# First pair's features before attention, later pairs' features at row blocks' ends, in a two-layer graph attention kernel

## The chip, the cores and the metric

The kernel runs on one core of a Trainium2 chip. The core has five engines that run side by side, each working through its own instructions in order: PE (matrix multiply, with its weight loads shown apart as PEld), DVE (vector), ACT (activation functions), POOL (a slower general engine) and SP, which here only issues DMAs. They meet at semaphores. The metric is the device time of one execution in microseconds (us), the median of several runs.

## The reference

There are N = 4096 nodes with 512 columns each, and an adjacency matrix of 4096 x 4096 floats. Two layers of attention follow each other, both with a layer norm, a ReLU and a residual:

```
h = relu(layernorm(x))                       # no scale, no shift
d = (h @ W.T + b).reshape(N, 8, 64)          # features of 8 heads
src, trg = sum(d * src_proj), sum(d * trg_proj)        # [N, 8] each
e = leaky_relu(src[n] + trg[m]) + adj[n, m]            # per head, [N, N]
x = x + softmax(e) @ d                                 # layer 0

h = relu(layernorm(x))
k, q, v = h @ Wk, h @ Wq, h @ Wv             # 8 heads of 64
a = softmax(q k^T / 8 - 1e16 * (1 - max(adj, eye)))
x = x + sum over heads of (a @ v) @ Wo                 # layer 1
```

Everything is in fp32. Only layer 0 is touched by the change.

## The kernel before, in words

Heads are taken in pairs. Layer 0 handles the first three pairs (`PAIRS` = 3) in one loop and the fourth in a loop of its own, into which the projections of layer 1 are woven; then comes layer 1's attention and a last product with `Wo`. All loops are written out in the order in which each engine is to work (`manual_schedule`); tiles come from pools with a fixed number of buffers, and a tile waits until the one before it in its buffer is done with.

**The prologue** (L394 to L417) works in sets of four row blocks (512 nodes), eight sets, each step of a set one iteration behind the one before:
- `load_rows` loads 1 MB of `x` into one of three buffers, `moments` takes mean and variance on DVE.
- `normed` makes (x - mean) * rstd, half of it on DVE and half on POOL (L309).
- `turned_rows` turns it on PE (L321), and ACT takes it out of PSUM with a ReLU as `hT` (L324). All eight `hT` stay in SBUF for the features.
- `halves` needs no features: `prepared` has multiplied the weights with the projections into a small matrix `u` (16 columns), and `u` times `hT` gives the source and target half of every logit (L332, 16 rows by 512 columns). The target halves go to DRAM (`trg_d`) and come back spread over all partitions as `tb`; the source halves are turned into columns (`sources`, L346).
- at the end `turned_weights` turns the weights on PE into `wt`.

**The attention loop** (L425 to L464) takes a group, a block of 128 rows of one head pair, in two steps, one per head, and each step in two half steps. 96 groups make 192 steps. In a step n:
- `leaky` (ACT, L143) makes the 128 x 4096 leaky sums into a tile `t`; it is issued one step ahead, in half step 0.
- `masked` (DVE, L154) adds 2048 columns of `adj` per half step and takes the smallest (L159).
- `exps` (ACT, L164) follows one step behind, in half step 1.
- `turned` (PE, L177) transposes a quarter of the group per half step, `taken` copies it out of PSUM in two tiles, two of seven on ACT (L186), the rest on DVE (L188); `weighted` (PE, L199) multiplies the quarter of the half step before with the features. `LEAD` = 7 half steps lie between a step and its transposes; `t` has 7 buffers.
- `finish` ends a group in three further half steps: the sums are copied (L212), turned back on PE (L217), divided by the denominators and added to the block of `x` (L220, L223), and stored to `x1_d`.

The features of all pairs are made in the first eight half steps of that loop (`features`, L357, one set per half step, 256 matmul records in all), get their bias on DVE (`features_out`, L365) and go to DRAM as `d1_d` (L368). `load_feats` (L131) brings one pair's quarter at a time back into one of four buffers. SP issues all these DMAs in the written order, so that one that waits holds up those behind it.

Of the kernel before, what the change touches and what calls it, by code (L numbers as in the profile page):

```python
# [23 lines left out]
def kernel(  # L24
# [49 lines left out]
    x1_d = dram.tile([N, DM], F32, name="x1_d")  # L74
    qk_d = dram.tile([P, HC, 2, N], F32, name="qk_d")
# [12 lines left out]

    CH = 2048
# [6 lines left out]
    LEAD = 7  # L96
    with tc.tile_pool(name="a0k", bufs=1) as pk, tc.tile_pool(name="a0v", bufs=4) as pv, tc.tile_pool(
        name="a0a", bufs=3
    ) as pa, tc.tile_pool(name="a0t", bufs=7) as pt, tc.tile_pool(name="a0p", bufs=4) as pp, tc.tile_pool(
        name="a0x", bufs=1  # L100
    ) as px, tc.tile_pool(name="a0s", bufs=4) as psb, tc.tile_pool(
# [3 lines left out]
        class Group:  # L105


            def __init__(self, c, g):
                self.c, self.g = c, g
                self.t = {}  # L110
                self.nm = {}
                self.pT = {}

# [78 lines left out]
        def weighted(G, i):  # L192
            if i == 0:
                G.o = po.tile([P, 2 * P], F32, name="o")
            for b in range(MB):
                mb = i * MB + b
                pT = G.pT[i, b // 4]
                for h in range(2):
                    nc.tensor.matmul(  # L199
                        G.o[h * D : (h + 1) * D, :P],  # L200
                        lhsT=feats[G.c][i][:, b, bass.ts(h, D)],
                        rhs=pT[:, bass.ts(b % 4 * 2 + h, P)],
                        start=(mb == 0), stop=(mb == NB - 1),
                    )

        def finish(G):

            rows, cols = bass.ts(G.g, P), bass.ts(G.c, PR)
            xt = px.tile([P, PR], F32, name="xt")
            nc.sync.dma_start(xt, x[rows, cols])  # L210
            oT = px.tile([P, P], F32, name="oT")
            nc.vector.tensor_copy(oT, G.o[:, :P])  # L212
            den = psb.tile([P, 2], F32, name="den")
            nc.vector.reciprocal(den, G.sm)
            yield
            back = G.o[:, P:]
            nc.tensor.transpose(back, oT, ident)  # L217
            yield
            att = px.tile([P, 2, D], F32, name="att")
            nc.vector.tensor_mul(  # L220
                att, back.rearrange("p (h d) -> p h d", d=D), den.unsqueeze(2).to_broadcast([P, 2, D])
            )
            nc.gpsimd.tensor_add(xt, xt, att.rearrange("p h d -> p (h d)"))  # L223
            nc.sync.dma_start(x1_d[rows, cols], xt)

        XR = CH // DM
        u = px.tile([P, P], F32, tag="oT", name="u")[:, : KC * 2 * H].rearrange("p (c k) -> p c k", c=KC)
# [16 lines left out]
        def prepared(wn, col):  # L244


            by_head = px.tile([P, 2, D], F32, tag="att", name="by_head").rearrange("p a d -> p (a d)")
            by_head = by_head[:, : HC * 2 * H].rearrange("p (c k) -> p c k", c=HC)
            nc.vector.memset(by_head, 0.0)
            for c in range(HC):  # L250
                for half in range(2):
                    rows = bass.ts(half, D)
                    at = 2 * c + half
                    nc.vector.tensor_copy(by_head[rows, c, at : at + H + 1 : H], col[rows, 0:2, c])
            up = ptr.tile([P, TW], F32, tag="tr", name="up")
            for kc in range(KC):
                for c in range(HC):
                    nc.tensor.matmul(
                        up[:, bass.ts(kc, 2 * H)], lhsT=wn[c // 2][:, c % 2, bass.ts(kc, P)], rhs=by_head[:, c],
                        start=(c == 0), stop=(c == HC - 1),  # L260
                    )
            for c in range(HC):
                nc.tensor.matmul(
                    up[: 2 * H, 512:513], lhsT=by_head[:, c], rhs=col[:, 2, c : c + 1],
                    start=(c == 0), stop=(c == HC - 1),
                )
            nc.vector.tensor_copy(u.rearrange("p c k -> p (c k)"), up[:, : KC * 2 * H])
            nc.vector.tensor_copy(cs[: 2 * H], up[: 2 * H, 512:513])

        def turned_weights(wn):  # L270
            wt = []
            for j in range(KC // 2):
                tp = ptr.tile([P, TW], F32, tag="tr", name="wtp")
                for i in range(2):
                    for c in range(HC):
                        nc.tensor.transpose(
                            tp[:, bass.ts(i * HC + c, P)], wn[c // 2][:, c % 2, bass.ts(j * 2 + i, P)], ident
                        )
                wt.append(pv.tile([P, 2, HD], F32, tag="v", name="wt"))
                nc.scalar.copy(wt[j].rearrange("p k o -> p (k o)"), tp)  # L280
            return wt
# [21 lines left out]
        def normed(R):  # L303
            nc.vector.reciprocal(R.rstd, R.rstd)
            R.hn = []
            for r in range(XR):
                if r % 2 == 0:
                    R.hn.append(pp.tile([P, 2, DM], F32, tag="pT", name="hn"))
                (nc.gpsimd if r % 2 else nc.vector).tensor_scalar(  # L309
                    R.hn[-1][:, r % 2], R.x[:, r], R.mv[:, r, 0:1], R.rstd[:, r], ALU.subtract, ALU.mult  # L310
                )

        def turned_rows(R, q):
# [3 lines left out]
            for j in range(XR // 2):  # L317
                tp = ptr.tile([P, TW], F32, tag="tr", name="htp")
                for r in range(2):
                    for kc in range(KC):  # L320
                        nc.tensor.transpose(  # L321
                            tp[:, bass.ts(r * KC + kc, P)], R.hn[j][:, r, bass.ts(kc, P)], ident
                        )
                nc.scalar.activation(  # L324
                    R.hT[:, bass.ts(j, 2)].rearrange("p r k n -> p (r k n)"), tp, AF.Relu
                )

        def halves(R, q):

            lp = ptr.tile([P, TW], F32, tag="tr", name="lp")  # L330
            for kc in range(KC):
                nc.tensor.matmul(  # L332
                    lp[: 2 * H, : XR * P], lhsT=u[:, kc], rhs=R.hT[:, :, kc, :],
                    start=(kc == 0), stop=(kc == KC - 1),
                )
            R.lr = pp.tile([P, TW], F32, tag="pT", name="lr")
            nc.vector.tensor_scalar(
                R.lr[: 2 * H, : XR * P], lp[: 2 * H, : XR * P], cs[: 2 * H], None, ALU.add
            )
            nc.sync.dma_start(trg_d[:, bass.ts(q, XR * P)], R.lr[H : 2 * H, : XR * P])  # L340

        def sources(R, q):

            sp = po.tile([P, 2 * P], F32, tag="o", name="sp")
            for r in range(XR):
                nc.tensor.transpose(  # L346
                    sp[:, bass.ts(r, H)], R.lr[:H, bass.ts(r, P)], ident[:H, :H]
                )
            nc.vector.tensor_copy(
                src[:, bass.ts(q, XR), :].rearrange("p n h -> p (n h)"), sp[:, : XR * H]  # L350
            )

        def features(R, q, j):
            tp = ptr.tile([P, TW], F32, tag="tr", name="mp")
            for r in range(2):
                for kc in range(KC):
                    nc.tensor.matmul(  # L357
                        tp[:, bass.ts(r, HD)], lhsT=R.hT[:, j * 2 + r, kc, :], rhs=wt[kc // 2][:, kc % 2, :],
                        start=(kc == 0), stop=(kc == KC - 1),
                    )  # L360
            return tp

        def features_out(q, j, tp):
            d1 = pp.tile([P, 2, HD], F32, tag="pT", name="d1")
            nc.vector.tensor_add(  # L365
                d1, tp.rearrange("p (r o) -> p r o", r=2), bb.unsqueeze(1).to_broadcast([P, 2, HD])
            )
            nc.sync.dma_start(  # L368
                d1_d[bass.ts(q * XR // 2 + j, 2 * P), :].rearrange("(r p) d -> p r d", p=P), d1
# [23 lines left out]
        with tc.manual_schedule():  # L393
# [5 lines left out]
            for q in range(NQ + 4):  # L399
                if q + 2 < NQ:  # L400
                    rows.append(load_rows(q + 2))
                if q < NQ:
                    moments(rows[q])
                if q == 1:
                    prepared(wn, col)
                if 0 <= q - 1 < NQ:
                    normed(rows[q - 1])
# [10 lines left out]
            wt = turned_weights(wn)  # L418
            bb = pk.tile([P, HD], F32, name="bb")
            nc.sync.dma_start(bb, b0.partition_broadcast(P))  # L420
# [4 lines left out]
            for s in range(total + 6):  # L425
                G, h = step(s) if s < total else (None, 0)
                for half in range(2):
# [8 lines left out]
                    q = 2 * s + half  # L436
                    made = [(q, j, features(rows[q], q, j)) for j in range(XR // 2)] if q < NQ else []
                    if q == NQ + 1:
                        sources_by_sets()
                    if half == 0 and s + 1 < total:  # L440
# [5 lines left out]
                    if half == 1 and 0 <= s - 1 < total:  # L446
                        exps(*step(s - 1))
                    if s < total:
                        masked(G, h, half)
                    for each in made:  # L450
                        features_out(*each)
                    if q < NQ and q % 2:
                        load_feats(0, q // 2)
# [4 lines left out]
                    if 1 <= n <= 2 * total:  # L458
                        W, w = groups[(n - 1) // HALVES], (n - 1) % HALVES
                        weighted(W, w)  # L460
                        if W.g == NB - 1 and W.c + 1 < PAIRS:
# [629 lines left out]
```

## Time and profile before

| what | us |
|---|---|
| median of 3 runs | 5093.84 (5091.9 to 5098.46) |
| the profiled execution | 5095.06 |
| its span, first to last instruction | 5093.2 |
| prologue, to the first `leaky` | 92.57 |
| from there to the fourth `exps` | 120.97 |
| last weighted sum of layer 0's loop starts | 1802.07 |
| busy in the whole span: PE, DVE, ACT, POOL | 4812.7, 4541.1, 3928.1, 376.7 |

A row of a timeline gives start, duration, engine, line, operation, output and inputs, shapes and how many were merged; in brackets the idle time of the engine before it and what ended it. Durations of neighbouring instructions overlap at their ends, so the distance from one start to the next is the better price. A row of a group list gives line, engine, operation, tiles, shapes, count, then busy us and mean ns of one, then the idle time before them. One fp32 matmul makes two records on PE.

### The profile page before, as it was taken

To read this page: it belongs to the slowest core of one execution; us is meant where nothing else is said; L and a number is where in the kernel's file an instruction comes from. 1 tells how busy PE (TensorE), PEld (TensorE's weight loads), DVE (VectorE), ACT (ScalarE), POOL (GpSimd) and SP (SyncE) were. 2 spreads that over 40 slices of the span, in tenths; PEclk is the share of its full clock that TensorE was granted. 3 is DMA by queue.
4 is the path that set the end of the run, shared out by engine and by line. 5 is a ranking of instruction groups with operands and counts; after the bars stand their busy time and mean duration, and the time that the engine had idled before them with its cause. 6 is when DMAs were issued, how large, how long until landed. Compare 5 with 4: busy or idle time off the path is not lost.

```text
span 5093.2 us, 145280 instructions
## 1 busy us (share of the span) xinstructions
PE 4812.7 (94%) x61850; PEld 3471.2 (68%) x61850; DVE 4541.1 (89%) x8125; ACT 3928.1 (77%) x4581; POOL 376.7 (7%) x632
## 2 busy tenths in 40 slices
PE   7999999999999959999989999999999999999999
PEld 3588888888888847677756666666666666666664
DVE  4599999999999989888759999999999999999971
ACT  3499999999999988888748888666666666666651
POOL 2000000000000011111112222000000000000000
PEclk9999999999999979999999999999999999999999
DMA  4344353344443364444367777544343343533325
GB/s 157 129 142 140 127 190 132 134 142 169 147 142 128 126 161 136 138 142 138 107 205 239 240 239 239 167 128 127 126 159 126 125 126 128 157 125 126 127 94 178
DMA packets 316152, 764.83 MB, mean 150 GB/s; under 512 B 54448, under 2 KB 156848, under 8 KB 290416
## 3 DMA queue, kind: packets, MB, share of 16 engines
q1 hardware_dynamic: 314976, 754.49, 46.1%
q8 instruction: 486, 7.96, 0.7%
q14 instruction: 162, 1.33, 0.1%
q10 hardware_dynamic: 528, 1.05, 0.1%
HBM read 629.41 MB, written 125.96 MB: 148 GB/s over the span
## 4 chain that ended last, share of the span: by engine, by line
PE 55%; DVE 20%; ACT 14%; issue 7%; DMA 4%; SPq 1%; POOL 0%; DVEq 0%; ACTq 0%; POOLq 0%
PE o L937 18%; PE sc L856 18%; DVE t L154 6%; DVE pT L188 6%; PE tr L920 6%; ACT t L143 4%; ACT t L164 3%; DVE bt L557 3%; PE oo L1058 2%; ACT pT L186 2%; PE mp L357 2%; PE tr L177 2%; DVE bt L596 2%; PE o L199 2%; ACT bt L589 1%
## 5 line engine op out<-in xcount | busy, mean ns | idle before, releaser
L872 DVE CUSTOM_DVE_ANT_0 t<-sc,a 128x512 f32<-128x512 f32 x2048 | 1291.4, 686 | 77.3 <-issue 55.3
L907 ACT ACTIVATE t<-t,nm 128x1024 f32<-128x1024 f32 x1024 | 1168.5, 1143 | 163.7 <-DVE nm L896 163.7
L937 PEld LDWEIGHTS o<-t,v 128*64 128x64 f32 x16384 | 883.9, 137 | 423.7 <-issue 337.7
L856 PE MATMUL sc<-k,q 64*32 64x512 f32 x16384 | 1003.1, 597 | 9.4 <-DVE nm L872 9.4
L937 PE MATMUL o<-t,v 128*64 128x128 f32 x16384 | 1007.1, 276 | 0.2 <-ACT oT L947 0.2
L914 DVE STREAM_TRANSPOSE t<-t 128x1536 f32<-128x1536 f32 x512 | 908.2, 1774 | 8.9 <-ACT t L907 5.9
L154 DVE CUSTOM_DVE_ANT_0 t<-t,a 128x2048 f32<-128x2048 f32 x384 | 876.5, 2282 | 18.0 <-DMA a<-in_adj_dram 18.0
L177 PE MATMUL tr<-ident,t 128*128 128x128 f32 x6144 | 782.6, 277 | 103.3 <-ACT pT L186 91.9
L164 ACT ACTIVATE t<-t,nm 128x4096 f32<-128x4096 f32 x192 | 786.7, 4097 | 27.5 <-DVE nm L159 27.5
L143 ACT ACTIVATE t<-tb,src 128x4096 f32<-128x4096 f32 x192 | 786.2, 4096 | 19.0 <-PE mp L357 17.4
L177 PEld LDWEIGHTS tr<-ident,t 128*128 128x128 f32 x6144 | 664.0, 141 | 198.8 <-ACT pT L186 115.1
L199 PE MATMUL o<-pT,v 128*64 128x128 f32 x12288 | 757.1, 276 | 0.3 <-DVE pT L188 0.3
L199 PEld LDWEIGHTS o<-pT,v 128*64 128x64 f32 x12288 | 664.4, 137 | 64.0 <-issue 63.0
L188 DVE COPY pT<-tr 128x1024 f32<-128x1024 f32 x549 | 657.4, 1217 | 40.4 <-PE tr L177 33.5
L926 ACT COPY t<-tr 128x512 f32<-128x512 f32 x512 | 299.1, 584 | 483.4 <-PE tr L920 478.6
L856 PEld LDWEIGHTS sc<-k,q 64*32 64x32 f32 x16384 | 251.2, 106 | 342.0 <-issue 299.6
L920 PE MATMUL tr<-ident,t 128*128 128x128 f32 x2048 | 342.7, 287 | 10.9 <-ACT t L907 9.2
L547 ACT ACTIVATE lk<-tb,srcb 128x1024 f32<-128x1024 f32 x256 | 281.9, 1112 | 80.8 <-DVE nm L557 73.9
L186 ACT COPY pT<-tr 128x1024 f32<-128x1024 f32 x219 | 302.6, 1382 | 52.1 <-DMA d_d<-d 36.1
L596 DVE STREAM_TRANSPOSE bt<-bt 128x2048 f32<-128x2048 f32 x128 | 295.1, 2306 | 30.0 <-ACT bt L589 30.0
L557 DVE CUSTOM_DVE_ANT_0 bt<-lk,ba 128x1024 f32<-128x1024 f32 x256 | 302.1, 1215 | 22.0 <-ACT e L681 11.2
L589 ACT ACTIVATE bt<-bt,nm 128x1024 f32<-128x1024 f32 x256 | 290.3, 1135 | 0.4 <-DVE nm L578 0.3
(113 smaller groups left out, 3911.2 us busy)
## 6 DMA issues: line engine op xcount, KB each, us to landing
a<-in_adj_dram SPq DMA_DIRECT2D x192, 1024.0 KB, 5.6
a<-pen_d SPq DMA_DIRECT2D x384, 512.0 KB, 3.8
ba<-in_adj_dram SPq DMA_DIRECT2D x512, 128.0 KB, 2.9
a<-in_adj_dram SPq DMA_DIRECT2D x512, 128.0 KB, 3.3
pen_d<-a SPq DMA_DIRECT2D x128, 512.0 KB, 3.4
qk_d<-e SPq DMA_DIRECT2D x64, 256.0 KB, 2.2
x<-in_x_dram SPq DMA_DIRECT2D x8, 1024.0 KB, 5.7
d_d<-d SPq DMA_DIRECT2D x16, 512.0 KB, 2.9
```

What stands on the lines that cost most here:

```text
L143: nc.scalar.activation(t, targets[G.c, h], AF.Prelu, bias=src[:, G.g, 2 * G.c + h : 2 * G.c + h + 1], alpha=SLOPE)
L154: nc.vector.tensor_tensor_reduce(out=t, in0=t, in1=rows_of_adj[G, f], scale=-1.0, scalar=FMAX, op0=ALU.add, op1=ALU.min, accum_out=nm[:, f ...
L164: nc.scalar.activation(G.t[h], G.t[h], AF.Exp, bias=G.nm[h][:, NCH : NCH + 1], scale=-1.0, accum_out=G.sm[:, h : h + 1],)
L177: nc.tensor.transpose(tr[:, bass.ts(b % 4 * 2 + h, P)], G.t[h][:, bass.ts(i * MB + b, P)], ident)
L188: nc.vector.tensor_copy(pT, tr)
L199: nc.tensor.matmul(G.o[h * D : (h + 1) * D, :P], lhsT=feats[G.c][i][:, b, bass.ts(h, D)], rhs=pT[:, bass.ts(b % 4 * 2 + h, P)], start=(mb ...
L856: nc.tensor.matmul(sc[h][bass.ts(a, SQ), :], lhsT=G.q[bass.ts(h, D), bass.ds(G.q0 + k * SQ, SQ)], rhs=keys[G.c][half][bass.ts(h, D), a, :] ...
L872: nc.vector.tensor_tensor_reduce(out=t[:, G.ring + k, h, cols], in0=scs[half][h], in1=a[:, cols], scale=1.0, scalar=FMAX, op0=ALU.add, op1 ...
L907: nc.scalar.activation(u, u, AF.Exp, bias=G.nm[k // 2][:, k % 2, h : h + 1], scale=-1.0, accum_out=G.sm[:, k, h : h + 1],)
L914: nc.vector.transpose(u, u)
L920: nc.tensor.transpose(tr[:, bass.ts(h * NT + m, P)], t[:, G.ring + k, h, bass.ds(VC + m * P, P)], ident)
L937: nc.tensor.matmul(G.o[bass.ts(h, D), :P], lhsT=v[:, b, bass.ts(h, D)], rhs=t[:, bass.ds(G.ring, GS), h, bass.ds(at, SQ)], start=(mb == 0) ...
```

## The change

- **Features.** The eight `hT` are also stored to DRAM (`hT_d`), in the prologue. The first pair's features (128 of 512 columns) are made in the prologue, one set per iteration (`first_features`), and stay in SBUF. Those of the next pair are made during a pair's groups: `finish` multiplies one row block's `hT`, loaded back from DRAM (`load_rows_turned`), with 128 columns of `wt` right after the turn back, adds the bias and stores the 128 x 128 result to `d1_d`. Groups 0 and 1 of a pair do two blocks, groups 30 and 31 none.
- **Weights.** `turned_weights` moves to the second iteration of the prologue; `wt` and the bias get tiles of their own.
- **Logit halves.** `u` gets 32 columns per chunk (16 of them zero). Each of the four row blocks of a set has its own column tile of PE: 16 matmuls of 128 columns into 32 PSUM rows each, instead of 4 of 512 columns. One transpose makes the sources instead of four; four small stores write the targets instead of one.
- **Normalization.** All four blocks of a set go to POOL, as x * rstd + shift instead of (x - mean) * rstd; DVE makes the shift column.
- **Order.** `leaky` moves from half step 0 to 1 and `exps` from 1 to 0; `LEAD` and the buffers of `t` go from 7 to 6. The sources of the last pair are spread in step 1 instead of step 4.

```diff
-    LEAD = 7
+    LEAD = 6
...
-        name="a0t", bufs=7
+        name="a0t", bufs=6
...
+                self.blocks = [b for b in (g, NB - 2 + g) if b < (NB if g < 2 else NB - 2)]
...
+        def load_rows_turned(G):
+            G.hT = []
+            for b in G.blocks:
+                h = ph.tile([P, KC, P], F32, name="h")
+                nc.sync.dma_start(h, hT_d[b].rearrange("p (k n) -> p k n", k=KC))
+                G.hT.append(h)
...
             nc.tensor.transpose(back, oT, ident)
+            for i in range(len(G.blocks)):
+                for kc in range(KC):
+                    nc.tensor.matmul(
+                        G.o[:, bass.ts(2 + i, P)], lhsT=G.hT[i][:, kc, :], rhs=wt[:, kc, after],
+                        start=(kc == 0), stop=(kc == KC - 1),
+                    )
...
+            for i, b in enumerate(G.blocks):
+                d1 = px.tile([P, PR], F32, name="d1")
+                nc.vector.tensor_add(d1, G.o[:, bass.ts(2 + i, P)], bb[:, after])
+                nc.sync.dma_start(d1_d[bass.ts(b, P), after], d1)
...
-                (nc.gpsimd if r % 2 else nc.vector).tensor_scalar(
-                    R.hn[-1][:, r % 2], R.x[:, r], R.mv[:, r, 0:1], R.rstd[:, r], ALU.subtract, ALU.mult
+                nc.gpsimd.tensor_scalar(
+                    R.hn[-1][:, r % 2], R.x[:, r], R.rstd[:, r], R.shift[:, r], ALU.mult, ALU.add
...
+            nc.sync.dma_start(
+                hT_d[bass.ts(q, XR)].rearrange("r p k -> p r k"), R.hT.rearrange("p r k n -> p r (k n)")
+            )
...
             for kc in range(KC):
-                nc.tensor.matmul(
-                    lp[: 2 * H, : XR * P], lhsT=u[:, kc], rhs=R.hT[:, :, kc, :],
-                    start=(kc == 0), stop=(kc == KC - 1),
-                )
+                for r in range(XR):
+                    nc.tensor.matmul(
+                        lp[bass.ts(r, SQ), :P], lhsT=u[:, kc], rhs=R.hT[:, r, kc, :],
+                        start=(kc == 0), stop=(kc == KC - 1),
+                    )
...
+            for r in range(XR):
+                nc.sync.dma_start(
+                    trg_d[:, bass.ts(q * XR + r, P)], R.lr[r * SQ + H : r * SQ + 2 * H, :]
+                )
...
+        def first_features(R, q):
+            tp = ptr.tile([P, TW], F32, tag="tr", name="mp")
             for r in range(XR):
                 for kc in range(KC):
                     nc.tensor.matmul(
-                        tp[:, bass.ts(r, HD)], lhsT=R.hT[:, j * 2 + r, kc, :], rhs=wt[kc // 2][:, kc % 2, :],
+                        tp[:, bass.ts(r, PR)], lhsT=R.hT[:, r, kc, :], rhs=wt[:, kc, :PR],
...
+            nc.sync.dma_start(bb, b0.partition_broadcast(P))
-            for q in range(NQ + 4):
+            for q in range(NQ + 5):
...
+                if 0 <= q - 1 < NQ:
+                    normed(rows[q - 1])
                 if q == 1:
                     prepared(wn, col)
-                if 0 <= q - 1 < NQ:
-                    normed(rows[q - 1])
+                    turned_weights(wn)
...
-                    made = [(q, j, features(rows[q], q, j)) for j in range(XR // 2)] if q < NQ else []
-                    if q == NQ + 1:
+                    if (s, half) == (1, 0):
                         sources_by_sets()
-                    if half == 0 and s + 1 < total:
+                    if half == 0 and 0 <= s - 1 < total:
+                        exps(*step(s - 1))
+                    if half == 1 and s + 1 < total:
                         leaky(*step(s + 1))
...
-                    if half == 1 and 0 <= s - 1 < total:
-                        exps(*step(s - 1))
...
                         weighted(W, w)
+                        if w == 0:
+                            load_rows_turned(W)
```

## The prediction

> **What bounds the kernel now.** I read the busy times by stretch first. Columns: stretch, its length, then busy time and count on PE, PEld, DVE, ACT, POOL, then granted clock, DMA share, GB/s.
>
> ```profile
> 0.00:92.57 92.57, 66.10 (x286) 35.12 (x287) 43.31 (x118) 20.51 (x27) 37.27 (x23) 0.98 0.45 146
> 92.57:213.50 120.93, 115.60 (x311) 54.35 (x311) 42.53 (x40) 35.62 (x14) 0.00 (x0) 0.98 0.38 139
> 300.00:1740.00 1440.00, 1345.56 (x16689) 1203.43 (x16687) 1402.84 (x1622) 1440.00 (x718) 42.09 (x87) 1.00 0.41 144
> ```
>
> Three stages touch the change: a prologue without attention (to 92.57, the first leaky), a stretch in which PE is full and ACT works 36 of 121 us, and the steady attention of the first three pairs, in which ACT never rests. The rest of the span is another stage's code and is not touched. The timeline of ACT shows what the second stretch is:
>
> ```profile
> 92.57 10.91 ACT L143 ACTIVATE t<-tb,src 128x4096 f32<-128x4096 f32 x3 [1.62 <-DMA tb<-trg_d]
> 107.83 1.28 ACT L164 ACT_TABLE_LOAD   x1 [4.35 <-DVE nm L159]
> ...
> 145.33 3.72 ACT L143 ACTIVATE t<-tb,src 128x4096 f32<-128x4096 f32 x1 [6.22 <-PE mp L357]
> 162.78 3.71 ACT L164 ACTIVATE t<-t,nm 128x4096 f32<-128x4096 f32 x1 [13.73 <-DVE nm L159]
> ...
> 212.63 1.01 ACT L186 COPY pT<-tr 128x1024 f32<-128x1024 f32 x1 [36.12 <-DMA d_d<-d]
> 213.54 3.71 ACT L164 ACTIVATE t<-t,nm 128x4096 f32<-128x4096 f32 x1
> ```
>
> Up to the fourth exp (213.54) ACT waits for features (mp L357) and what is queued behind them. Last, the timeline of the steady state, where start-to-start distances are the real prices:
>
> ```profile
> 1005.08 4.12 ACT L164 ACTIVATE t<-t,nm 128x4096 f32<-128x4096 f32 x1
> 1007.52 2.28 DVE L154 CUSTOM_DVE_ANT_0 t<-t,a 128x2048 f32<-128x2048 f32 x1
> 1007.84 1.97 PE L177 MATMUL tr<-ident,t 128*128 128x128 f32 x16
> ...
> 1008.78 4.10 ACT L143 ACTIVATE t<-tb,src 128x4096 f32<-128x4096 f32 x1
> ...
> 1011.12 2.28 DVE L154 CUSTOM_DVE_ANT_0 t<-t,a 128x2048 f32<-128x2048 f32 x1
> 1011.63 1.97 PE L177 MATMUL tr<-ident,t 128*128 128x128 f32 x16
> 1012.39 1.39 ACT L186 COPY pT<-tr 128x1024 f32<-128x1024 f32 x1
> 1013.28 4.11 ACT L164 ACTIVATE t<-t,nm 128x4096 f32<-128x4096 f32 x1
> ...
> 1013.52 2.35 DVE L188 COPY pT<-tr 128x1024 f32<-128x1024 f32 x2
> ...
> 1015.78 2.28 DVE L154 CUSTOM_DVE_ANT_0 t<-t,a 128x2048 f32<-128x2048 f32 x1
> ...
> 1016.98 4.11 ACT L143 ACTIVATE t<-tb,src 128x4096 f32<-128x4096 f32 x1
> ```
>
> Per group (two steps, four half steps), with 8 tiles out of PSUM, 2/7 of them on ACT:
> - ACT: exp 3.70, leaky 3.61, copy 0.89: 2 x 7.31 + 2.29 x 0.89 = 16.65. The exps run at 8.33 a step, so ACT sets the pace.
> - DVE: four masks of 2.21, two minima of 0.19, 5.71 copies of 1.13 and 0.47 of ends: 16.15.
> - PE: a half step of transposes and weighted sums is 1011.63 - 1007.84 = 3.79: with the turn back (0.11) 15.27.
>
> **The change, part by part.**
>
> *Features out of the first half steps.* 256 matmul records of L357 (110.6 us busy, 0.43 each for 512 columns) and 16 additions leave. From the first leaky to the fourth exp ACT then has only its own work: six leakys 21.7, three exps 11.1, table 1.3, a copy 0.9 = 35.0, and one wait, as the first exp needs both masks of step 0. The first mask now starts 5.9 after the leaky, because the first adj tile lands then; two masks are 4.6 and the second tile costs another 1.5, so the exp can start at 12, where leaky 0 and 1 end at 7.2: 4.8. The set of sources moved ahead of step 1's masks is about 1.5 on DVE and lies in the slack of step 1's exp. So 40 instead of 121: **81 us gained**. The new order does the fourth exp before the sixth leaky; I count the same work on both sides.
>
> *The prologue.* PE per four row blocks: 16 transposes 1.90; logit halves; one transpose 0.3 instead of four; first features 32 records of 128 columns at 0.43/4 = 0.107, 3.4. The halves were 8 records of 0.43 = 3.4; now 32 of 0.107 in four column tiles. No row has this form. Bounds: side by side 0.9, one after another 3.4; L856 runs eight tiles at 0.061 a record of 0.43, seven at once, so I take 1.0. Together 6.7, with the changes of mode 6.8. DVE falls to 4.4 (moments 3.2, small ones 0.6, feature addition 0.6).
>
> POOL now does four normalizations per block set instead of two. Its rows differ in price by the pair of operations:
>
> ```profile
> L843 POOL TENSOR_SCALAR a<-a 128x1024 f32<-128x1024 f32 x128 | 134.7, 1053 | 466.8 <-ACT a L842 297.1 <-DMA a<-in_adj_dram 156.1 <-DMA pen_d<-a 5.2
> L654 POOL TENSOR_SCALAR bhn<-xr,bmv,brstd 128x512 f32<-128x512 f32 x32 | 66.1, 2073 | 110.8 <-issue 87.3 <-DVE brstd L650 23.5
> L731 POOL TENSOR_SCALAR wq<-wq 128x2048 f32<-128x2048 f32 x1 | 5.4, 5378 | 0.0
> ```
>
> Subtract-multiply with two columns as operands is 2.07 per 512 elements, one multiply 1.34, add-multiply with constants 0.53. The new pair, multiply-add with columns, is in no row: between 0.53 and 2.07. Here a rule of the Trainium skill bears (GPSIMD Engine Reference, section 3.1): a tight loop with one input needs about 1.8 cycles an element, 0.77 us for 512. L654's row is nearly three times that. What decides is 6.8/4 = 1.7 us: below it PE sets the prologue, and three of four prices lie below; I take that.
> - PE sets it: `up` ends near 26 as now (17.1 start, plus 16 more records for the column sums), the weights' transposes 29.5, at the slow rate that this stretch shows (L258 and the first transposes 0.21 a record, later 0.11). Turned rows of sets 0 and 1, halves 0: 37; the first full set at 44; five more at 6.8: 78; the last halves 79. Today the last logit addition ends at 87.5 and the first leaky starts 5.1 later; three more issues to trg_d on SP add 1.1. First leaky at **85.5, 7 us earlier**.
> - At 2.07 POOL sets it: its second set can start at 30.4, since DVE stands in `prepared` until 26.9 (waiting for `up` on PE) and then has moments of 3.2; seven sets of 8.25 end at 88.1, then transposes 0.5, halves and features still queued ahead on PE 4.7, the last halves 1.0, 6.5 to the leaky: 101, **8.5 us later**.
>
> SP's queue in the prologue gets a hT store of 1 MB and four small stores per set, and bb ahead of the third x. Loads of x wait for a normalization there already; the new stores stand behind those loads, so only stores come late, and the last block of targets is what the leaky waits for. Bytes rise from 13.5 to about 22 MB in 86 us, 0.8 of what 0.45 busy at 146 GB/s makes of a full share. Hidden if x keeps its two sets of lead; up to 5 us if not.
>
> *Next pair's features at block ends.* Per group 4 matmuls = 8 records of 128 columns. Price 0.107 each (L357 by columns; the 16 transposes go at 0.11): 0.86 on PE, 15.27 to 16.13. DVE one addition of 128x128 from PSUM, 0.20 like L220: 16.35. ACT nothing, 16.65. Each stays under ACT, by 0.5 and 0.3 us; without that cover they would cost 0.86 and 0.20 times 96 groups, 83 and 19 us. On PE they stand ahead of the weighted sums, so that the next transposes come 0.9 later; ACT's copy of those comes after its own 3.6 us operation, and transposes wait for ACT's copies anyway (90 us in this stretch). Groups 0 and 1 do two blocks: DVE waits for one store there, some 2 us six times, within its margin. Loads of h go out five half steps ahead (256 KB, 20 GB/s more); on SP they stand ahead of an adj load that is due two steps later. The 64 KB stores of d1 wait for DVE just where the x1 store already waits for POOL.
>
> *Order and depth.* LEAD and buffers 7 to 6: leaky now runs one half step before its mask instead of two, exp one half step after its mask instead of two; transposes stay two behind exp, a t buffer two half steps free. Read from the timeline: step 100 has its masks at 1007.52 and 1011.12, minimum at 1013.6. In the new order its leaky takes ACT's slot 1005.08 to 1008.78 and its exp the slot at 1016.98. The first mask would start 1.3 late, the exp still has 3.4 - 1.3 = 2.1 us left. In the worst half step, with two copies on DVE, mask to minimum takes 6.9, against 7.3 on ACT plus its copies. So nothing is lost; a DVE 2 us later than this would cost.
>
> *Sum.* 81 + 7 = 88. The profiled execution took 5095.06 (span 5093.2), 0.02% over the runs' median 5093.84; from the median: **5006 us**.
>
> **Rivals.**
> - *POOL sets the prologue*, as computed: 81 - 8.5 = 72.5, 5021. For it: the only price with column operands. Against: price follows the pair.
> - *PE becomes the bound of the attention.* At 0.21 a record, as L258 shows for 128-wide weights, PE needs 15.27 + 1.7 = 17.0 a group, 0.3 over ACT, 90 groups: +30, 5035. Against it: in that stretch transposes too took 0.21, so it is the clock, not the load. It ends **slower than before** if loading and streaming follow each other, 0.21 + 0.107 = 0.32: 17.8 a group, 1.2 x 90 = 105, 5111. It decides from 88/90 = 0.98 us over 16.65: 0.30 a record.
> - *The change doesn't do what it says*: ACT's 121 us stay, because leaky or mask wait for something else (transfers): gain only some 30 us, 5065. Against: adj's first tile is the only other wait there.
>
> **Chances.** 5006: 0.57 (its own range 4992 to 5022). 5021: 0.22. PE at 5035: 0.08. Little gain, 5040 to 5085: 0.05. Within 0.2% (10 us, about what a measurement of this kernel can tell): 0.02. Slower: 0.06. Faster altogether 0.92. The range takes the first two whole, some of the third, and 10 us for transfers and first waits: 4990 to 5040.
>
> **What would show it.** Right: first leaky near 85, fourth exp 40 later; POOL's hn under 1.7 us; ACT again without idle time from there to the last exp and 8.33 a step; PE's waits for ACT's copies cut from 90 us to under 30. Wrong: hn at 2.07 and a leaky at 101; ACT waiting for DVE's minimum or for PE's transposes in the steady stretch; block-end records over 0.11.

## The result

The changed kernel takes **5033.26 us** (median of 4 runs, 5031.49 to 5033.83) against 5094.59 for the kernel before in the same session (4 runs, 5091.9 to 5098.46): a ratio of 0.9878, 95% interval 0.9861 to 0.9896. The forecast was 5006 with a range of 4990 to 5040. So the direction and the range hold, and the point is 27 us too low; 5033 also lies outside the 4992 to 5022 that the prediction gave its main case. The profiled execution took 5033.3, its span is 5031.5, and the span gained 61.7 us where the sum said 88.

The busy times of the kernel after by stretch (stretch, length, busy time and count on PE, PEld, DVE, ACT, POOL, granted clock, DMA share, GB/s), with 10 us out of the prologue at the end:

```profile
0.00:92.57 92.57, 62.65 (x598) 57.66 (x599) 36.55 (x110) 20.38 (x27) 24.93 (x39) 0.91 0.61 210
92.57:213.50 120.93, 95.97 (x1078) 87.17 (x1079) 95.85 (x116) 103.91 (x51) 1.38 (x3) 0.89 0.51 178
300.00:1740.00 1440.00, 1414.16 (x17307) 1277.92 (x17305) 1391.75 (x1683) 1414.04 (x706) 39.87 (x87) 1.00 0.46 160
60.00:70.00 10.00, 7.73 (x77) 7.17 (x77) 4.42 (x13) 2.12 (x3) 3.02 (x4) 0.84 0.79 268
```

ACT works 103.9 us of the second stretch where it worked 35.6. In the third, ACT's busy time falls short of 1440 because the loop now ends at 1737.8 and because of 4.6 us of idle time between 220 and 1700. The last row is new: in the middle of the prologue PE runs at a granted clock of 0.84, where the kernel before had 0.98 over its whole prologue.

ACT's timeline from the first leaky (L147) to the fourth exp (L168), start and duration first:

```profile
106.29 7.31 ACT L147 ACTIVATE t<-tb,src 128x4096 f32<-128x4096 f32 x2 [13.70 <-DMA tb<-trg_d]
115.56 1.28 ACT L168 ACT_TABLE_LOAD   x1 [1.97 <-DVE nm L163]
116.86 3.71 ACT L168 ACTIVATE t<-t,nm 128x4096 f32<-128x4096 f32 x1
...
139.64 3.72 ACT L168 ACTIVATE t<-t,nm 128x4096 f32<-128x4096 f32 x1
```

The stretch is 33.4 us. In the new order the fourth exp has one leaky fewer ahead of it, so 37 us is what compares with the 40 that I counted. But it starts at 106.29: the first leaky comes 13.7 us later than before (92.57), not 7 us earlier. Where the 26.3 us between 88 and 61.7 went: the fourth exp was at 213.54 and is at 139.64, which with 3.6 us for the missing leaky is a gain of 70.3 (17.7 short: 20.8 in the prologue, 3.1 back in the stretch); the steady stretch, from the fourth exp to the 189th, grew from 1540.26 to 1547.75 (7.5 lost); what follows lost about 1, for a reason that was not looked for.

PE's timeline of the prologue shows the first of these. L348 are the transposes, L363 the logit halves, L387 the first pair's features, one set after the other:

```profile
44.34 6.67 PE L387 MATMUL mp<-wt,hT 128*128 128x128 f32 x32 [5.22 <-ACT hT L351]
50.84 1.91 PE L348 MATMUL htp<-ident,hn 128*128 128x128 f32 x16
52.68 1.08 PE L363 MATMUL lp<-hT,u 128*32 128x128 f32 x32
56.30 5.46 PE L387 MATMUL mp<-wt,hT 128*128 128x128 f32 x32 [2.27 <-ACT hT L351]
...
77.79 5.36 PE L387 MATMUL mp<-wt,hT 128*128 128x128 f32 x32 [2.27 <-ACT hT L351]
82.99 1.91 PE L348 MATMUL htp<-ident,hn 128*128 128x128 f32 x16
84.83 1.08 PE L363 MATMUL lp<-hT,u 128*32 128x128 f32 x32
86.01 3.74 PE L387 MATMUL mp<-wt,hT 128*128 128x128 f32 x32
...
92.60 3.74 PE L387 MATMUL mp<-wt,hT 128*128 128x128 f32 x32
```

From one set's features to the next it is 10.75 us (56.30, 67.04, 77.79). In a long set PE waits 2.27 us for ACT's hT, and the 32 feature records then take 5.46 instead of 3.74: together 3.99, which is the distance from my 6.8. From 86.01 PE goes through without a wait, and a set takes 6.6 us. The very first features, at 44.34, lose more: a wait of 5.22, and 6.67 for the records. The halves' 32 records of 1.08 us are the 1.0 that I took.

The other engines in one of the long sets, from the same timeline:

```profile
61.80 0.69 DVE L393 TENSOR_TENSOR v<-mp,bb 128x512 f32<-128x512 f32 x1 [6.11 <-PE mp L387]
62.41 0.68 DVE L320 BATCH_NORM_STATS2 stats<-x 128x6 f32<-128x512 f32 x1
...
65.60 0.14 DVE L326 RECIPROCAL rstd<-rstd 128x4 f32<-128x4 f32 x1
65.78 0.30 ACT L323 ACTIVATE rstd<-mv,eps 128x4 f32<-128x4 f32 x1 [8.63 <-DVE rstd L326]
65.99 1.92 ACT L351 ACTIVATE hT<-htp 128x1024 f32<-128x1024 f32 x2
66.20 3.02 POOL L336 TENSOR_SCALAR hn<-x,rstd,shift 128x512 f32<-128x512 f32 x4 [7.74 <-DVE shift L329]
67.04 5.46 PE L387 MATMUL mp<-wt,hT 128*128 128x128 f32 x32 [2.27 <-ACT hT L351]
...
72.55 0.69 DVE L393 TENSOR_TENSOR v<-mp,bb 128x512 f32<-128x512 f32 x1 [6.11 <-PE mp L387]
```

Read it as a ring, a chain of waits that comes back to its own start. DVE's addition waits for the features; the four moments of the next set stand behind it on DVE; ACT's square root (L323) waits for them, and the ReLUs (L351), whose input PE had finished long before, stand behind the square root on ACT; the features wait for a ReLU. Then it starts again. The transposes and halves (3 us) are the only PE work beside the moments. The loss of clock has its place in the ring too, as rows of 2 us show:

```profile
56.00:58.00 2.00, 1.71 (x11) 1.71 (x12) 0.00 (x0) 1.16 (x2) 2.00 (x4) 0.78 0.36 139
58.00:60.00 2.00, 2.00 (x12) 2.00 (x11) 0.00 (x0) 0.00 (x0) 0.47 (x1) 0.50 1.00 332
60.00:62.00 2.00, 2.00 (x17) 2.00 (x17) 0.20 (x1) 0.00 (x0) 0.00 (x0) 0.86 0.80 194
62.00:64.00 2.00, 2.00 (x34) 1.83 (x36) 1.93 (x5) 0.00 (x0) 0.00 (x0) 1.00 0.87 284
```

The features start at 56.30 and meet the low clock right behind the wait. If it is one stretch at 0.50, the rows make it 2 x (0.22 + 0.50 + 0.14) / 0.50 = 3.4 us long, and half of that, 1.7, is what the records take too long.

The next pair's features in a group of the steady stretch, between the turn back (L229) and the weighted sums (L203):

```profile
1011.38 0.27 PE L229 MATMUL o<-ident,oT 128*128 128x128 f32 x1
1011.49 1.06 PE L232 MATMUL o<-wt,h 128*128 128x128 f32 x8
1012.48 1.97 PE L203 MATMUL o<-pT,v 128*64 128x128 f32 x32
```

Turn back and features together hold PE for 1.10 us, where the turn back alone held it for 0.20 (L217 at 1013.44 to L199 at 1013.64 in the kernel before): 0.90 more.

In the steady stretch, waits of the kernel after between 300 and 1700 (us in total, times, longest):

```profile
PE tr L181 <- ACT pT L190: 19.0, 48, 1.5
DVE t L158 <- ACT t L147: 18.4, 40, 0.9
DVE d L244 <- DMA d_d<-d: 9.0, 4, 2.9
...
ACT t L168 <- DVE nm L163: 4.4, 3, 2.0
```

Read from one exp to the next, the 7.5 us that the steady stretch lost are in few places. In the kernel before, exps follow each other at 8.2 or 9.1 us throughout; here the same holds but for six that come 0.2 to 2.1 us late, one near 190 (1.5 us) and five at the starts of the second and third pair (5.7 in all).

### The profile page after: what moved, and what is told of

Its sections match the earlier page's. It is cut to its first block, busy times and chain, and to the rows that moved or that the text cites. A ratio compares the mean times of both kernels' runs of the same rounds, so it can differ in the third digit from the quotient of the medians.

```text
span 5031.5 us, 147684 instructions
## 1 busy us (share of the span) xinstructions
PE 4802.4 (95%) x62810; PEld 3552.2 (71%) x62810; DVE 4530.7 (90%) x8205; ACT 3929.0 (78%) x4581; POOL 362.1 (7%) x648
## 3 DMA queue, kind: packets, MB, share of 16 engines
HBM read 652.48 MB, written 132.25 MB: 156 GB/s over the span
## 4 chain that ended last, share of the span: by engine, by line
PE 46%; DMA 1%; ACT 1%; issue 1%; DVE 1%; SPq 0%; POOL 0%; ACTq 0%; DVEq 0%; POOLq 0%
PE o L959 18%; PE sc L878 18%; PE tr L942 6%; PE oo L1080 2%; DMA a<-in_adj_dram 1%; ACT t L929 1%; PE nmB L913 1%; PE den L972 0%; DVE t L936 0%; PE back L979 0%; SPq L852 0%; PE mp L697 0%; DVE t L894 0%; ACT aT L1077 0%; PE mpv L709 0%
## 5 line engine op out<-in xcount | busy, mean ns | idle before, releaser
L181 PEld LDWEIGHTS tr<-ident,t 128*128 128x128 f32 x6144 | 665.4, 141 | 130.6 <-issue 65.5
L203 PE MATMUL o<-pT,v 128*64 128x128 f32 x12288 | 756.8, 276 | 0.8 <-DVE pT L192 0.8
L147 ACT ACTIVATE t<-tb,src 128x4096 f32<-128x4096 f32 x192 | 732.0, 3813 | 13.7 <-DMA tb<-trg_d 13.7
L168 ACT ACTIVATE t<-t,nm 128x4096 f32<-128x4096 f32 x192 | 731.7, 3811 | 6.9 <-DVE nm L163 6.6
L203 PEld LDWEIGHTS o<-pT,v 128*64 128x64 f32 x12288 | 664.1, 137 | 60.7 <-issue 46.9
L942 PEld LDWEIGHTS tr<-ident,t 128*128 128x128 f32 x2048 | 213.7, 140 | 111.3 <-issue 85.0
```

What stands on the lines that cost most here:

```text
L147: nc.scalar.activation(t, targets[G.c, h], AF.Prelu, bias=src[:, G.g, 2 * G.c + h : 2 * G.c + h + 1], alpha=SLOPE)
L168: nc.scalar.activation(G.t[h], G.t[h], AF.Exp, bias=G.nm[h][:, NCH : NCH + 1], scale=-1.0, accum_out=G.sm[:, h : h + 1],)
L181: nc.tensor.transpose(tr[:, bass.ts(b % 4 * 2 + h, P)], G.t[h][:, bass.ts(i * MB + b, P)], ident)
L203: nc.tensor.matmul(G.o[h * D : (h + 1) * D, :P], lhsT=feats[G.c][i][:, b, bass.ts(h, D)], rhs=pT[:, bass.ts(b % 4 * 2 + h, P)], start=(mb ...
L942: nc.tensor.transpose(tr[:, bass.ts(h * NT + m, P)], t[:, G.ring + k, h, bass.ds(VC + m * P, P)], ident)
```

## The experiments

All are timed against the kernel before on the same chip: the first four kernels against 5093.56, the other four against 5093.14. The changed kernel was timed once, against 5094.59, so differences from it below carry 1 to 2 us from the kernel before alone. The ratios' intervals of the changed kernel and of those 7 us below it touch; their runs do not overlap. What decides is where the time goes in the profiles (starts in us):

| kernel | median | first leaky | 4th exp | 189th exp |
|---|---|---|---|---|
| changed | 5033.26 | 106.29 | 139.64 | 1687.39 |
| ReLU ahead | 5025.73 | 98.37 | 132.06 | 1679.64 |
| hT stored later | 5037.59 | 103.10 | 144.12 | 1692.55 |
| two result tiles | 5026.18 | 106.06 | 139.31 | 1679.90 |
| both mends | 5019.73 | 98.51 | 132.25 | 1673.06 |
| old pair on POOL | 5037.18 | 109.09 | 142.94 | 1690.99 |
| product twice | 5069.99 | 104.25 | 137.78 | 1719.71 |
| two queues | 5021.84 | 97.32 | 131.56 | 1672.30 |

A profile's first leaky is not steadier than some 2 us: two of these kernels have the changed prologue unaltered, those with two result tiles and with the product made twice.

**ReLU ahead of the square root.** The transposes and ReLUs of a set are written ahead of the moments of the set two later, so that ACT no longer holds the ReLU behind the square root.

```diff
                     rows.append(load_rows(q + 2))
+                if 0 <= q - 2 < NQ:
+                    turned_rows(rows[q - 2], q - 2)
                 if q < NQ:
                     moments(rows[q])
...
-                if 0 <= q - 2 < NQ:
-                    turned_rows(rows[q - 2], q - 2)
```

> The changed kernel with the turned rows and their ReLU put ahead of the moments in each iteration of the prologue; nothing else. Theory (a chain in series): in the changed kernel's prologue a set takes 10.75 us because first features 5.4, their addition 0.7, moments 3.1, small ones 0.45 and the ReLU 1.05 follow each other: ACT stands at the square root, which waits for the moments, which DVE does only after the addition, and the ReLU behind it frees the PSUM tile for the next features. Then a set falls to 7 to 8 us and the first leaky comes at 92 to 97 instead of 106.3: 5020 to 5025 instead of 5033. Rival (transfers: the stores of hT crowd out x): sets stay at 10 us or more and the time at 5030 to 5036.

Measured: **5025.73** (5024.77 to 5029.11), 0.9868 (0.9853 to 0.9882): 7.5 under the changed kernel, first leaky at 98.37. Its timeline:

```profile
54.99 3.74 PE L387 MATMUL mp<-wt,hT 128*128 128x128 f32 x32
...
62.38 3.74 PE L387 MATMUL mp<-wt,hT 128*128 128x128 f32 x32
...
65.92 0.69 DVE L320 BATCH_NORM_STATS2 stats<-x 128x6 f32<-128x512 f32 x1 [5.17 <-DMA x<-in_x_dram]
...
76.14 3.84 PE L387 MATMUL mp<-wt,hT 128*128 128x128 f32 x32
```

These features run at full clock and without a wait: the ring was the cause of both. The first features, too, now start at 39.48 instead of 44.34. The time is 0.7 over the expected range. Sets take 6.6 to 8.9 us but for one. The leaky is 1.4 us later than I had expected because that one takes 13.8: its moments wait 5.17 for a block of x that was issued at 57.23 and was there at 65.9, with two hT stores issued right after it and the DMA engines busy to 0.97 between 60 and 70. So with the ring gone transfers seem to come next; a kernel with this edit and without those stores was not run.

**hT stored later.** The 1 MB stores of hT leave the prologue; they are issued in the first half steps of attention instead.

```diff
+        def store_turned(q):
+            R = rows[q]
             nc.sync.dma_start(
...
                         load_adj(groups[s // 2 + 1], h)
+                    if s < 2:
+                        for q in (4 * s + 2 * half, 4 * s + 2 * half + 1):
+                            store_turned(q)
```

> The changed kernel with the eight stores of hT moved out of the prologue into the first four half steps of the attention; nothing else. Theory (chain in series): sets stay at 10.7 us; only the small stores of the targets no longer stand behind a hT store on SP, so the first leaky comes 0 to 3 us earlier, 5030 to 5034. Rival (transfers: 8 MB of stores crowd out x and the targets): sets fall to 7 us and the first leaky to 86 to 92, 5014 to 5020.

Measured: **5037.59** (5036.09 to 5038.85), 0.989 (0.9874 to 0.9907). The timeline, on PE, ACT and DVE:

```profile
66.03 5.47 PE L390 MATMUL mp<-wt,hT 128*128 128x128 f32 x32 [2.27 <-ACT hT L351]
...
103.10 7.31 ACT L147 ACTIVATE t<-tb,src 128x4096 f32<-128x4096 f32 x2 [11.49 <-DMA tb<-trg_d]
...
119.27 3.71 ACT L147 ACTIVATE t<-tb,src 128x4096 f32<-128x4096 f32 x1 [1.21 <-DMA hT_d<-hT]
...
133.33 2.29 DVE L158 CUSTOM_DVE_ANT_0 t<-t,a 128x2048 f32<-128x2048 f32 x1 [8.03 <-DMA a<-in_adj_dram]
...
135.92 3.71 ACT L168 ACTIVATE t<-t,nm 128x4096 f32<-128x4096 f32 x1 [5.65 <-DVE nm L163]
```

With 8 MB fewer in the prologue the sets are the same 10.75 us with the same 2.27 of waiting, so transfers were not what made them long. The time missed the expected 5030 to 5034, though. The leaky gains 3.2 at the prologue's end, and more than that is given back, as from there to the fourth exp it takes 41.0 instead of 33.4: a leaky waits for a tile that is still being stored, and a mask waits 8 us for an adj tile issued behind the stores, which is the exp's 5.65.

**Two result tiles.** The features of the two blocks at a group's end get a tile each.

```diff
-                d1 = px.tile([P, PR], F32, name="d1")
+                d1 = px.tile([P, PR], F32, tag=f"d1{i}", name="d1")
```

> The changed kernel with a buffer of its own for each of the two d1 tiles of a group; nothing else. Theory: in groups 0 and 1 of each pair the second addition waits 2 to 3 us for the store of the first, masks come late, and ACT stands idle some 4.6 us at the starts of pairs 1 and 2 and 2 to 3 us at pair 0's: 5026, 7 us less, and no idle ACT between 220 and 1650. Rival (the time is lost to the order of leaky and exp): unchanged within 2 us.

Measured: **5026.18** (5023.93 to 5029.41), 0.9868 (0.9853 to 0.9883), 7.1 under the changed kernel, and no wait of ACT is left between 220 and 1700. What it removes is this, in the changed kernel's timeline at the second pair's group 0:

```profile
716.52 0.28 DVE L244 TENSOR_TENSOR d<-o,bb 128x128 f32<-128x128 f32 x1
...
716.83 2.31 SPq L245 DMA_DIRECT2D d_d<-d  x2
718.50 0.29 DVE L244 TENSOR_TENSOR d<-o,bb 128x128 f32<-128x128 f32 x1 [1.69 <-DMA d_d<-d]
718.71 1.21 DVE L192 COPY pT<-tr 128x1024 f32<-128x1024 f32 x1
719.84 2.28 DVE L158 CUSTOM_DVE_ANT_0 t<-t,a 128x2048 f32<-128x2048 f32 x1
...
726.83 3.72 ACT L168 ACTIVATE t<-t,nm 128x4096 f32<-128x4096 f32 x1 [2.03 <-DVE nm L163]
```

DVE idles 1.69 for the first tile's store; the copies and masks behind it are late, PE's transposes with them, and ten us later the exp is 2.03 late. With two tiles all six late exps are gone: the fourth to the 189th take 1540.59 us, against 1547.75 in the changed kernel and 1540.26 in the kernel before.

**The order alone.** The kernel before, with leaky and exp exchanged between the half steps; depth and buffers stay at 7.

```diff
-                    if half == 0 and s + 1 < total:
+                    if half == 0 and 0 <= s - 1 < total:
+                        exps(*step(s - 1))
+                    if half == 1 and s + 1 < total:
                         leaky(*step(s + 1))
...
-                    if half == 1 and 0 <= s - 1 < total:
-                        exps(*step(s - 1))
```

> The kernel before with leaky and exp exchanged between the half steps, LEAD and buffers left at 7; nothing else. Theory: ACT keeps 8.33 us a step and no idle time in the steady stretch: 5090 to 5098. Rival (the slack taken from DVE is what cost 7 us in the steady stretch): 5100 or more, with ACT waiting for the minimum.

Measured: 5095.14 (12 runs, 5091.76 to 5098.0), 1.0003 (0.9994 to 1.0012). ACT is busy 1440.00 of 1440 us, as before. The order costs nothing. The depth of 6 was not tried alone, but the kernel with both mends below has it, and its steady stretch is 1540.81 us.

**Both mends**, the ReLU's place and the two tiles, in the changed kernel.

> The changed kernel with both edits of the earlier runs: the ReLU ahead of the moments, and two d1 tiles. Theory (two separate losses): they add, 7.9 in the first leaky and 7.1 in the steady stretch: 5018 to 5020. Rival (the first edit moves work so that the second is already hidden): 5024 or more.

Measured: **5019.73** (5017.85 to 5021.4), 0.9854 (0.9839 to 0.9869), 13.5 under the changed kernel. The two losses are separate: 7.5 + 7.1 = 14.6, and the 189th exp comes 14.3 earlier. No kernel here has a lower median. The stretch of 1380 us from 300, first the changed kernel:

```profile
300.00:1680.00 1380.00, 1356.55 (x16585) 1225.61 (x16584) 1347.59 (x1628) 1375.37 (x684) 37.59 (x82) 1.00 0.47 164
```

and the kernel with both mends, where ACT never rests:

```profile
300.00:1680.00 1380.00, 1359.97 (x16652) 1230.46 (x16652) 1353.59 (x1636) 1380.00 (x687) 38.00 (x83) 1.00 0.47 164
```

**POOL with the old pair of operations.**

```diff
-                    R.hn[-1][:, r % 2], R.x[:, r], R.rstd[:, r], R.shift[:, r], ALU.mult, ALU.add
+                    R.hn[-1][:, r % 2], R.x[:, r], R.mv[:, r, 0:1], R.rstd[:, r], ALU.subtract, ALU.mult
```

> The changed kernel with the normalization's pair of operations as before, subtract and multiply with two columns, still all on POOL; the shift column is made but not used. Theory: the price on POOL goes by the pair, so one normalization takes 2.07 us instead of 0.77; a set then holds POOL for 8.3 us, which lies inside the chain of 10.75: first leaky 0 to 4 us later, 5033 to 5037. Rival (all of POOL's work lies on the path): 4 x 1.3 x 8 = 42 us later.

Measured: 5037.18 (5035.65 to 5038.85), 0.9889 (0.9873 to 0.9906), 3.9 over the changed kernel; first leaky at 109.09. Group rows (busy, mean ns of one, idle before), of the changed kernel:

```profile
L336 POOL TENSOR_SCALAR hn<-x,rstd,shift 128x512 f32<-128x512 f32 x32 | 24.2, 770 | 61.8 <-DVE shift L329 42.5 <-DMA x<-in_x_dram 15.0 <-PE htp L348 4.4
```

and of this one:

```profile
L336 POOL TENSOR_SCALAR hn<-x,mv,rstd 128x512 f32<-128x512 f32 x32 | 65.9, 2072 | 28.3 <-DVE rstd L326 20.4 <-DVE shift L329 7.9
```

Same engine, same shape, both with two columns as operands: 770 ns against 2072, where DVE took 546 for the old pair (L309 of the kernel before). The price goes by the pair of operations; that the columns come from other tiles too was not tried apart. The time is about as expected, but not for the reason expected: the dear pair does not hide inside the ring. In this profile PE's transposes wait 10.9 us in all for POOL (hn L336) and its features only 3.7 for ReLUs, where those of the changed kernel wait 12.0. POOL has largely taken the ring's place, at about the same length: from the first features to the sixth it is 47.8 us, against 48.3 in the changed kernel, and they start 5.2 later.

**The product made twice.** At every group's end each matmul of the next pair's features is issued twice over, one result on top of the other; the computed values stay what they were.

```diff
-            for i in range(len(G.blocks)):
+            for i in [i for i in range(len(G.blocks)) for _ in range(2)]:
```

> The changed kernel with each block-end feature product made twice into the same place, the second one counting; nothing else. Theory (the sums of a group): PE needs 16.13 + 0.86 = 17.0 us a group where ACT needs 16.65, so PE becomes the pace for some 90 groups: +25 to +35 us, 5058 to 5068, with ACT waiting for transposes. Rival (PE has more slack than the sum says): under +8 us.

Measured: **5069.99** (5068.05 to 5071.56), 0.9953 (0.9938 to 0.9967): 36.7 over the changed kernel, just over the expected top of 35. Its busy times:

```profile
300.00:1680.00 1380.00, 1377.83 (x16866) 1271.69 (x16865) 1324.42 (x1589) 1348.86 (x669) 36.58 (x80) 1.00 0.47 161
```

and ACT's group of copies in the same stretch:

```profile
L190 ACT COPY pT<-tr 128x1024 f32<-128x1024 f32 x185 | 186.3, 1007 | 29.8 <-PE tr L181 29.8
```

PE is full and ACT now waits for its transposes. The fourth to the 189th exp take 1581.93 us, 34.2 more than in the changed kernel; the expected sum, 0.34 a group over ACT's 16.65, makes 31 over 90 groups. So the margin is as thin as the sum has it.

**Small stores from two queues.** Both mends, and every second of the small target stores is issued by ACT.

```diff
-                nc.sync.dma_start(
+                (nc.scalar if r % 2 else nc.sync).dma_start(
                     trg_d[:, bass.ts(q * XR + r, P)], R.lr[r * SQ + H : r * SQ + 2 * H, :]
```

> The changed kernel with the ReLU ahead of the moments, two d1 tiles, and every second small store of the targets issued from ACT's queue instead of SP's. Theory: SP's stores of the last two sets take 7.6 us in a row and the last targets wait for them; two queues halve that: 2 to 3 us below the version without it, 5015 to 5018. Rival (the stores wait for earlier transfers to land, not for SP): within 1 us of it, or slower, as ACT then stands behind the logit addition.

Measured: 5021.84 (5019.72 to 5023.21), 0.9858 (0.9843 to 0.9873): no gain over both mends. The last small stores in SP's queue with both mends:

```profile
86.15 7.38 SPq L370 DMA_DIRECT2D trg_d<-lr  x8
```

and with two queues:

```profile
86.02 6.50 SPq L370 DMA_DIRECT2D trg_d<-lr  x4
```

Half the issues take nearly the same time, so their number does not set the end. The profiles put part of both rows to waits for earlier transfers: 2.3 us for a store of hT with one queue, 4.8 for an earlier small store with two. That is inferred from the order of events, and no run removes it.

## Why the prediction was right, and where its sum was off

- *Direction and mechanism* were right: the stretch of 121 us, for most of which ACT waited for features, is 37 us on the same count of work, against the predicted 40.
- *The number* is in part luck. 5033 is nearest to 5035, the rival in which PE becomes the bound, and that did not happen: in the steady stretch ACT stands idle some 6 us in all, and not for PE. The range held because rivals had been taken into it. Of the prediction's own signs, `hn` at 0.77 and PE's waits of 19.0 are among those for right; a leaky past 101 and ACT's waits for DVE's minimum are among those for wrong.
- **The prologue** is the step that failed: "PE sets it", "five more at 6.8", "First leaky at 85.5, 7 us earlier". PE's own prices were right (1.91, 1.08 and 3.74 at full clock make 6.7). What failed is that "DVE falls to 4.4" was laid beside PE's 6.8. The parts stand in a ring through the queues of DVE and ACT: features, addition, moments, square root, ReLU, features. It closes because the feature addition stands ahead of the next moments on DVE, and the square root ahead of the ReLUs on ACT. Moving the ReLUs opened it: sets without a wait run at full clock, and the time fell by 7.5.
- *Where its 20.8 us are*: the first full set ends at 51.0, not 44 (7.0); five more take 45.3, not 34 (11.3); and from the last halves (97.35) to the leaky it is 8.9, not 6.5 (2.4). The first of these is the ring with a late transfer in it. ReLUs stand behind moments, and these wait 3.96 for a block of x (DVE at 39.69). Its load had to wait on SP until POOL had normalized the second set (issued at 33.54). The prediction had that set on POOL only from 30.4 on, but did not follow it to the load.
- Within the ring, 1.7 us of each long set are **the clock**, as worked out above. The Trainium skill (TensorE: Matmul & The Clock Gate, Part 1) says that PE goes to half rate after an idle window of about 3.4 us. A wait of 4.29 with the ReLU first agrees (the transposes behind it take 3.68 instead of 1.91). The waits of 2.27 are shorter than that window, and still some 3.4 us at 0.50 followed each. The measurement decides: how much of a window may be idle is not shown by these runs.
- *Transfers*, "Hidden if x keeps its two sets of lead; up to 5 us if not": x kept its lead but for that one block. With the ring gone another set waits 5.17 for x. The three more small stores of a set were put at 1.1 us; the last four held SP's queue for 3.00 (from 97.86), 1.7 of it a wait for a store of hT by the profile, and that is most of the 2.4.
- *POOL* was right, 0.77 where the prediction took "under 1.7". The rival that POOL sets the prologue came nearer in time (5021) and is refuted in its cause; with the dear pair the kernel takes 3.9 more.
- *Groups 0 and 1*, "some 2 us six times, within its margin": the size of a wait was right (up to 2.9), the margin was not. It compared DVE's 16.35 per group with ACT's 16.65, an average; a wait of 2 us does not fit into 0.3. It cost 7.1.
- *Next pair's features* take 0.90 a group, predicted 0.86. Waits of PE for ACT's copies fell from 89.9 to 19.0 (between 300 and 1740, and 300 and 1700), predicted under 30. The rival that PE becomes the bound was one doubled product away. One argument against it is not shown: that the 0.21 a record of L258 "is the clock". The granted clock of that stretch is 1.00 in the profile (20 to 25), though 0.21 is also what records of this shape take at 0.50 (44.34: 6.67 for 32).
- *Order* was right: 1.0003 alone; the mask waits up to 0.9 for its leaky where 1.3 was expected.

Taken together, 88 - 20.8 + 3.1 - 7.5 - 1.1 = 61.7, the gain of the span; the last 1.1 is what remained, and has no cause here.

## What to carry to other kernels

Work that is added to a software pipeline is not costed by taking the busiest engine: write down for each engine what stands ahead of what in its queue, and follow one set around until it meets itself; the length of that ring is the price. A margin per group is an average, and a wait is paid at one place: hold it against the slack of that place, and where a second tile would remove the wait, give it one.

## What was not expected of the hardware

- POOL does a multiply-add with two columns in 770 ns for 128 x 512 and a subtract-multiply in 2072. The Trainium skill (GPSIMD Engine Reference, section 3.1) has 0.77 us for a tight loop; the first pair meets it to the digit, the second does not.
- PE lost clock with one wait of 2.27 us in each 10.75: about 3.4 us at 0.50 behind each, a mean of 0.84.
- From the first of eight stores of 4 KB to the end of the last it took 7.38 us on SP's queue, waits included, and 6.50 for four of them with the other four on another queue.
